# Linear attention with a routed expert layer: pairs of chunks, values held twice, and the next head's projection in alternating steps

## The chip, the cores and the metric

The kernel runs on one core of one Trainium2 chip. The metric is the device time of one execution in microseconds (us); the time before is the median of three runs. In the profile PE is the matmul engine (TensorE), PEld its weight loads, DVE VectorE, ACT ScalarE, POOL GpSimd, and SP (SyncE) a queue that issues most of the DMAs.

## The reference

One transformer layer on 2048 tokens of 512 numbers, in float32: a linear attention with 16 query heads in groups of four that share a key and a value head, and then a mixture of 32 experts, to which each token is sent by its eight best router choices.

```python
x = layernorm(x0)
q = rope(x @ Wq.T)            # 16 heads of 128
k = rope(x @ Wk.T)            # 4 heads of 128, each shared by 4 query heads
v = x @ Wv.T
qf, kf = elu(q) + 1, elu(k) + 1
for s in range(2048):         # a running state for each head
    state += kf[s][:, None] * v[s][None, :]
    z     += kf[s]
    out[s] = (qf[s] @ state) / (qf[s] @ z + 1e-6)
x1 = x0 + out @ Wo.T
# experts: softmax of the router's 64 logits, top 8 with a bias; of these, numbers below 32
# are experts with at most 256 tokens each (silu(gate) * up, then down), the others add
# their weight to a factor on the sum
return x1 + moe(layernorm(x1))
```

## The kernel before, in words

The first part, attention, takes about 885 of the 1235 us; the second, the experts, is not touched by the change.

The 2048 tokens are cut into four blocks `sb` of 512, each block into four chunks `c` of 128, each chunk into two halves of T = 64. The heads are worked off in four groups `g`; "head" below means such a group, one key head with its R = 4 query heads.

For each block the rows are normalised and transposed to `xT` (`norm_block`, transposes `pxt` at L262), and at g = 0 the values are projected for all four chunks (`values`, `pv` at L271, copied to `va` on ACT).

`project(sb, g, xT)` makes one head's inputs. The key projection is four matmuls into `pk` (L305), and `rope_feature` (L282 to L288) applies the rotation and elu + 1: five steps on DVE, an exponential on ACT (L287), one more step on DVE. `zT` is the running sum of the keys by a scan on DVE (L309). The four query projections `pq` (L317) follow, each with a `rope_feature`. Keys and queries share the two PSUM banks of `p_pj`. Then the denominators: DVE multiplies queries by `zT` (`qz`, L325), PE sums these into `pd` (L328), DVE adds 1e-6 and takes the reciprocal (`rd`, L331 and L332). They are needed along all partitions, so `rd` is stored to DRAM (`recip`, L333) and loaded back in four pieces, one per chunk, repeated for each partition (`rds`, L337). Both DMAs are issued by SP. `rds` has three buffers.

`attend(sb, g, c, ...)` works one chunk of one head:

- `by_token` has turned the keys to tokens by rows (transposes `pk` at L294, copied to `kk`).
- Scores `psc` of the two halves (L355) and new state terms `pst` (L361). The second state contains the first half's term, so the first matmul contracts over 64 rows and the second over 128. Both lie in one bank `psk`.
- DVE adds the old state (L366) and masks the scores to `at` (L370).
- For each half `po` is first the state times the queries (L376) and then the values times `at` (L379).
- DVE multiplies `po` by `rds` into `oT` (L381).

`output` multiplies the four `oT` of a chunk by `wo` (16 matmuls, `px`, L391) and adds the residual; `route` computes the router's logits, the top eight, and the ranks of the tokens in their experts by a matmul `pp` (L446 and L447), and `list_further` writes the token lists by indirect DMAs on POOL (L166).

The order of issue is written out in the loop at the end. At head g the whole projection of head g + 1 is issued first, then the four chunks of head g. At g = 3 the "next head" is head 0 of the next block, and the outputs and routes of earlier chunks stand between the chunks. [...] A scheduler may move instructions of independent parts against each other on an engine before they are fixed, so that parts of a chunk's work and of the projection stand among each other on PE and DVE.

Of the kernel before, what the change touches and what calls it, by code (L numbers as in the profile page):

```python
# [9 lines left out]
F32 = mybir.dt.float32  # L10
# [3 lines left out]
ALU = mybir.AluOpType  # L14
# [4 lines left out]
P = 128  # L19
# [3 lines left out]
G = 4  # L23
R = H // G
T = 64
# [27 lines left out]
def linattn_moe(  # L53
# [122 lines left out]
    with ExitStack() as ph:  # L176
        wts = ph.enter_context(tc.tile_pool(name="wts", bufs=1))
        blk = ph.enter_context(tc.tile_pool(name="blk", bufs=2))
# [3 lines left out]
        rdp = ph.enter_context(tc.tile_pool(name="rdp", bufs=NC - 1))  # L182
        rowp = ph.enter_context(tc.tile_pool(name="rowp", bufs=NC))
        vap = ph.enter_context(tc.tile_pool(name="vap", bufs=NC))
# [6 lines left out]
        p_sc = ph.enter_context(tc.tile_pool(name="p_sc", bufs=2, space=PSUM))  # L191
# [73 lines left out]

        def values(sb, c, xT):

            pv = p_pj.tile([P, G, HD], F32, tag="pj", name=f"pv_{sb}_{c}")
            pvf = pv.rearrange("p g d -> p (g d)")
            for k in range(KD):  # L270
                nc.tensor.matmul(pvf, lhsT=xT[:, k, ts(c, P)], rhs=wv[:, k, :],  # L271
                                 start=(k == 0), stop=(k == KD - 1))
            va = vap.tile([P, G, HD], F32, tag="va", name=f"va_{sb}_{c}")
            nc.scalar.copy(va, pv)
            return va
# [23 lines left out]
        def project(sb, g, xT):  # L299


            kT = qkp.tile([P, SB], F32, tag="kT", name=f"kT_{sb}_{g}")
            pk = p_pj.tile([P, SB], F32, tag="pj", name=f"pk_{sb}_{g}")
            for k in range(KD):
                nc.tensor.matmul(pk, lhsT=wk[:, k, ts(g, HD)], rhs=xT[:, k, :],  # L305
                                 start=(k == 0), stop=(k == KD - 1))
            rope_feature(kT, pk, sb, f"k{sb}_{g}")
            zT = zp.tile([P, SB], F32, tag="zT", name=f"zT_{sb}_{g}")
            nc.vector.tensor_tensor_scan(zT, ones[:, 0:1].to_broadcast([P, SB]), kT,  # L309
                                         zend[:, g : g + 1] if sb else 0.0, ALU.mult, ALU.add)  # L310
            if sb < NSB - 1:
                nc.scalar.copy(zend[:, g : g + 1], zT[:, SB - 1 :])
            qT = qkp.tile([P, R, SB], F32, tag="qT", name=f"qT_{sb}_{g}")
            for r in range(R):
                pq = p_pj.tile([P, SB], F32, tag="pj", name=f"pq_{sb}_{g}_{r}")
                for k in range(KD):
                    nc.tensor.matmul(pq, lhsT=wq[g][:, k, ts(r, HD)], rhs=xT[:, k, :],  # L317
                                     start=(k == 0), stop=(k == KD - 1))
                rope_feature(qT[:, r, :], pq, sb, f"q{sb}_{g}_{r}")

            pd = p_ms.tile([P, P], F32, tag="ms", name=f"pd_{sb}_{g}")
            for c in range(NC):
                cc = ts(c, P)
                qz = tmp.tile([P, R, P], F32, tag="qz", name=f"qz_{sb}_{g}_{c}")
                nc.vector.tensor_tensor(qz, qT[:, :, cc], zT[:, cc].unsqueeze(1).to_broadcast([P, R, P]),  # L325
                                        ALU.mult)
                for r in range(R):
                    nc.tensor.matmul(pd[ts(r, SL)], lhsT=pick[:, c, :], rhs=qz[:, r, :],  # L328
                                     start=(c == 0), stop=(c == NC - 1))
            rd = sml.tile([P, P], F32, tag="rd", name=f"rd_{sb}_{g}", bufs=1)  # L330
            nc.vector.tensor_scalar(rd, pd, 1e-6, None, ALU.add)  # L331
            nc.vector.reciprocal(rd, rd)  # L332
            nc.sync.dma_start(out=recip[sb][g].rearrange("r m t -> (r m) t"), in_=rd)  # L333
            rds = []
            for c in range(NC):
                t = rdp.tile([P, R, P], F32, tag="rds", name=f"rds_{sb}_{g}_{c}")
                nc.sync.dma_start(out=t, in_=recip[sb][g][:, c, :].unsqueeze(0).to_broadcast([P, R, P]))  # L337
                rds.append(t)
            return kT, qT, rds
# [3 lines left out]
        def attend(sb, g, c, proj, kk, va, oT):  # L343


            kT, qT, rds = proj
            n = f"{sb}_{g}_{c}"
            halves = range(P // T)
            half = [slice(c * P + a * T, c * P + (a + 1) * T) for a in halves]
            old = state[g]  # L350
            psk = p_sc.tile([P, R * T + 2 * HD], F32, tag="sc", name=f"psk_{n}")
            psc = psk[:, : R * T].rearrange("p (r t) -> p r t", r=R)
            pst = psk[:, R * T :].rearrange("p (a d) -> p a d", a=2)
            for a in halves:
                nc.tensor.matmul(psc[ts(a, T)], lhsT=kT[:, half[a]], rhs=qT[:, :, half[a]],  # L355
                                 start=True, stop=True)

            n_new = 2 if sb < NSB - 1 or c < NC - 1 else 1
            for a in range(n_new):
                to = slice(0, (a + 1) * T)  # L360
                nc.tensor.matmul(pst[:, a], lhsT=kk[to, c], rhs=va[to, g, :], start=True, stop=True)  # L361
            new = stp.tile([P, 2, HD], F32, tag=f"st{g}", name=f"state_{n}")
            if old is None:
                nc.vector.tensor_copy(new, pst)
            else:
                nc.vector.tensor_tensor(new[:, :n_new], pst[:, :n_new],  # L366
                                        old[:, 1:].to_broadcast([P, n_new, HD]), ALU.add)
            state[g] = new
            at = tmp.tile([P, R, T], F32, tag="at", name=f"at_{n}")
            nc.vector.tensor_tensor(at, psc, causal.unsqueeze(1).to_broadcast([P, R, T]), ALU.mult)  # L370
            pos = []
            for a in halves:
                po = p_o.tile([P, R, T], F32, tag=f"o{a}", name=f"po_{n}_{a}")
                before_half = (old[:, 1] if old is not None else None, new[:, 0])[a]
                if before_half is not None:
                    nc.tensor.matmul(po, lhsT=before_half, rhs=qT[:, :, half[a]], start=True, stop=False)  # L376
                pos.append((po, before_half is None))
            for a, (po, first) in enumerate(pos):
                nc.tensor.matmul(po, lhsT=va[ts(a, T), g, :], rhs=at[ts(a, T)], start=first, stop=True)  # L379
            for a, (po, first) in enumerate(pos):  # L380
                nc.vector.tensor_tensor(oT[:, :, half[a]], po, rds[c][:, :, ts(a, T)], ALU.mult)  # L381
# [22 lines left out]
        def route(ch, xw):  # L404
# [19 lines left out]
            sb_ = sml.tile([P, EZ], F32, tag="sbias", name=f"sbias_{ch}")  # L424
# [3 lines left out]
            rest = sml.tile([P, EZ], F32, tag="rest", name=f"rest_{ch}")  # L428
# [22 lines left out]
            if ch >= LISTED:  # L451

                free = sml.tile([P, E], F32, tag="hi", name=f"free_{ch}")
# [15 lines left out]
            hi = sml.tile([P, E], F32, tag="hi", name=f"hi_{ch}")  # L469
            nc.vector.tensor_scalar(hi, pos, float(C2), float(P * NCOL - 1), ALU.is_ge, ALU.mult)  # L470
            mi = sml.tile([P, E], F32, tag="mi", name=f"mi_{ch}")
            nc.vector.scalar_tensor_tensor(mi, pos, float(SL), off_2, ALU.is_ge, ALU.mult)
            ad = sml.tile([P, E], F32, tag="ad", name=f"ad_{ch}")
# [3 lines left out]
            ok = sml.tile([P, E], F32, tag="ok", name=f"ok_{ch}")  # L477
# [20 lines left out]
        projs = {(0, 0): project(0, 0, xTs[0])}  # L498
        oTs = {}
        waiting = []  # L500
        for sb in range(NSB):
# [3 lines left out]
            for g in range(G):  # L505
                if g == 0:
                    vas = [values(sb, c, xTs[sb]) for c in range(NC)]
                if g + 1 < G:
                    projs[sb, g + 1] = project(sb, g + 1, xTs[sb])
                elif not last:  # L510
                    xTs[sb + 1] = norm_block(sb + 1)
                    projs[sb + 1, 0] = project(sb + 1, 0, xTs[sb + 1])
                if last and g == G - 1:
                    for i in range(2):
                        load_pair(i)
                oT = otp.tile([P, R, SB], F32, tag="oT", name=f"oT_{sb}_{g}")
                oTs[sb, g] = oT
                kk = by_token(sb, g, projs[sb, g][0])
                for c in range(NC):
                    attend(sb, g, c, projs[sb, g], kk, vas[c], oT)  # L520
                    if g == G - 1:
                        if c != 1 and waiting:
                            route_and_list(*waiting.pop(0))
                        if c >= 1:
                            waiting.append((sb * NC + c - 1,
                                            output(sb, c - 1, [oTs[sb, i] for i in range(G)])))
# [23 lines left out]
        big = sml.tile([P, 2, 2, E // 2], F32, tag="big", name="big")  # L550
# [299 lines left out]
```

## Time and profile before

| | us |
|---|---|
| median of 3 runs | 1238.45 |
| lowest and highest of them | 1237.87 and 1241.02 |
| the profiled execution: its own time | 1237.05 |
| the profiled execution: span from first to last instruction | 1235.3 |
| PE busy in that span | 1050.5 |
| DVE busy | 637.9 |
| POOL busy | 219.7 |
| ACT busy | 130.2 |

The profile comes from one execution. Its page cuts the span into 40 slices of about 31 us and gives for each the busy share of every engine and the clock that was granted to TensorE. Windows give the same for any stretch; the timeline lists instructions with start and length, like ones put together with a count; the waits are listed by engine and line with what each wait ended on. L12 is line 12 of the kernel; the kernel after the change has other line numbers.

### The profile page before, as it was taken

What the parts mean: (1) busy time and instruction counts of PE and PEld (TensorE: products, weight loads), DVE (VectorE), ACT (ScalarE), POOL (GpSimd) and SP (SyncE); (2) the same over time, 40 slices, a digit from 0 to 9 for tenths busy, and PEclk for the clock granted to TensorE, in tenths of its full rate; (3) what the DMA queues carried; (4) which work ended last, traced back from release to release, by engine and by line L of the source; (5) the groups of instructions that cost most, each with busy time, mean ns of one, the idle gap of its engine ahead of it and who ended that gap; (6) DMA issues with size and microseconds to landing.
All of it is one profiled execution on the core that took longest, in us unless ns stands there. A gap on an engine that the chain in (4) does not pass through costs nothing. (4 is left out here: it accounts for less than half of the span.)

```text
span 1235.3 us, 13580 instructions
## 1 busy us (share of the span) xinstructions
PE 1050.5 (85%) x4410; PEld 530.9 (43%) x4410; DVE 637.9 (52%) x1553; ACT 130.2 (11%) x256; POOL 219.7 (18%) x254
## 2 busy tenths in 40 slices
PE   5999999999999899999999999999737765672772
PEld 2444444444444444444444444444312554441440
DVE  4888874358888435888843388834322111110110
ACT  1111110011121001112100111100011100110000
POOL 4000001430000343000034200023353121211211
PEclk9999999999999999999999999999967877786887
DMA  9411212100121210012321112340572484967224
GB/s 346 151 16 33 69 49 55 52 26 13 34 77 40 60 52 27 13 35 58 75 61 52 61 45 67 102 59 27 167 254 74 109 273 149 319 187 235 45 39 156
DMA packets 90840, 116.26 MB, mean 94 GB/s; under 512 B 12493, under 2 KB 47309, under 8 KB 90672
## 3 DMA queue, kind: packets, MB, share of 16 engines
q1 hardware_dynamic: 74640, 93.53, 25.5%
q0 software_dynamic: 10336, 12.51, 5.2%
q10 hardware_dynamic: 5760, 8.92, 2.0%
q8 instruction: 55, 0.90, 0.3%
q14 instruction: 49, 0.40, 0.1%
HBM read 101.35 MB, written 20.96 MB: 99 GB/s over the span
## 5 line engine op out<-in xcount | busy, mean ns | idle before, releaser
L317 PE MATMUL pq<-xT,wq 128*128 128x512 f32 x512 | 230.3, 599 | 10.1 <-DVE rb_q L284 10.1
L391 PE MATMUL px<-wo,oT 128*128 128x512 f32 x512 | 232.4, 599 | 0.0
L166 POOL DMA_INDIRECT slots<-tok,ai x120 | 117.6, 980 | 501.5 <-DVE ai L485 468.9
L317 PEld LDWEIGHTS pq<-xT,wq 128*128 128x128 f32 x512 | 94.4, 190 | 138.5 <-issue 107.3
L391 PEld LDWEIGHTS px<-wo,oT 128*128 128x128 f32 x512 | 93.9, 191 | 98.1 <-issue 97.6
L728 PE MATMUL pu<-xeT,gu 128*128 128x224 f32 (+1 forms) x352 | 69.4, 367 | 11.0 <-DVE xeT L656 9.7
L376 PE MATMUL po<-qT,state 128*128 128x256 f32 x248 | 76.8, 402 | 2.2 <-DVE oT L381 1.9
L728 PEld LDWEIGHTS pu<-xeT,gu 128*128 128x128 f32 x352 | 65.4, 230 | 15.4 <-issue 13.1
L393 DVE TENSOR_TENSOR x<-px,x 128x512 f32<-128x512 f32 x16 | 11.1, 692 | 113.6 <-PE px L391 98.8
L381 DVE TENSOR_TENSOR oT<-po,rds 128x256 f32<-128x256 f32 x128 | 50.1, 414 | 33.7 <-PE po L379 18.8
L305 PE MATMUL pk<-xT,wk 128*128 128x512 f32 x128 | 63.5, 627 | 0.7 <-ACT xT L263 0.7
L242 POOL TENSOR_TENSOR lnr<-lnv,mhalf 128x1 f32<-128x1 f32 (+1 forms) x20 | 13.3, 664 | 255.0 <-DVE lnv L240 228.8
L271 PE MATMUL pv<-wv,xT 128*128 128x512 f32 x128 | 57.7, 598 | 0.0
L361 PE MATMUL psk<-va,kk 64*128 64x128 f32 (+1 forms) x248 | 56.7, 323 | 0.0
L287 ACT ACTIVATE rb_q<-rb_q 128x512 f32<-128x512 f32 x64 | 40.3, 630 | 155.4 <-DVE rb_q L286 155.1
L376 PEld LDWEIGHTS po<-qT,state 128*128 128x128 f32 x248 | 41.2, 189 | 35.6 <-issue 21.7
L379 PE MATMUL po<-at,va 64*128 64x256 f32 x256 | 54.6, 428 | 0.0
L355 PE MATMUL psk<-qT,kT 128*64 128x256 f32 x256 | 50.5, 404 | 0.0
L361 PEld LDWEIGHTS psk<-va,kk 64*128 64x128 f32 (+1 forms) x248 | 36.8, 186 | 31.6 <-issue 23.8
L643 POOL DMA_INDIRECT acc<-y,idx x17 | 25.9, 1524 | 130.0 <-ACTq L778 40.0
L672 PE MATMUL pu_b<-gu,xeT_b 128*32 128x256 f32 x512 | 40.2, 424 | 10.0 <-issue 9.5
L325 DVE TENSOR_TENSOR qz<-qT,zT 128x512 f32<-128x512 f32 x64 | 42.4, 687 | 11.1 <-PE pd L328 10.6
(180 smaller groups left out, 1135.1 us busy)
## 6 DMA issues: line engine op xcount, KB each, us to landing
gu<-in_wgu_dram SPq DMA_DIRECT2D x32, 1024.0 KB
rds<-recip SPq DMA_DIRECT2D x64, 256.0 KB
dn<-in_wdn_dram SPq DMA_DIRECT2D x32, 512.0 KB
rows<-xw ACTq DMA_DIRECT2D x16, 272.0 KB
xn<-in_x_dram SPq DMA_DIRECT2D x16, 256.0 KB
wq<-in_wqT_dram SPq DMA_DIRECT2D x4, 1024.0 KB
wo<-in_woT_dram SPq DMA_DIRECT2D x4, 1024.0 KB
x<-in_x_dram SPq DMA_DIRECT2D x16, 256.0 KB
```

Of the source, the lines that this page charges most:

```text
L166: nc.gpsimd.indirect_dma_start(out=slots[k][:, :], out_offset=bass.IndirectOffsetOnAxis(ap=ai[:, k : k + 1], axis=0), in_=tok[:, ch : ch + 1],
L271: nc.tensor.matmul(pvf, lhsT=xT[:, k, ts(c, P)], rhs=wv[:, k, :], start=(k == 0), stop=(k == KD - 1))
L305: nc.tensor.matmul(pk, lhsT=wk[:, k, ts(g, HD)], rhs=xT[:, k, :], start=(k == 0), stop=(k == KD - 1))
L317: nc.tensor.matmul(pq, lhsT=wq[g][:, k, ts(r, HD)], rhs=xT[:, k, :], start=(k == 0), stop=(k == KD - 1))
L325: nc.vector.tensor_tensor(qz, qT[:, :, cc], zT[:, cc].unsqueeze(1).to_broadcast([P, R, P]), ALU.mult)
L355: nc.tensor.matmul(psc[ts(a, T)], lhsT=kT[:, half[a]], rhs=qT[:, :, half[a]], start=True, stop=True)
L361: nc.tensor.matmul(pst[:, a], lhsT=kk[to, c], rhs=va[to, g, :], start=True, stop=True)
L376: nc.tensor.matmul(po, lhsT=before_half, rhs=qT[:, :, half[a]], start=True, stop=False)
L379: nc.tensor.matmul(po, lhsT=va[ts(a, T), g, :], rhs=at[ts(a, T)], start=first, stop=True)
L381: nc.vector.tensor_tensor(oT[:, :, half[a]], po, rds[c][:, :, ts(a, T)], ALU.mult)
L391: nc.tensor.matmul(px, lhsT=oTs[h // R][:, h % R, ts(c, P)], rhs=wo[h // R][:, h % R, :], start=(h == 0), stop=(h == H - 1))
L728: nc.tensor.matmul(pu[:, a, :m], lhsT=weights[e][0][:, k, a, c, :], rhs=xeT[:, k, :m], start=(k == 0), stop=(k == KD - 1))
```

## The change

- *Pairs of chunks.* `attend` becomes `attending`, a generator that works two chunks together in two steps. The first step issues the four score matmuls of both chunks into one bank, the two state matmuls into another, the two additions of the state and the two masks. The second step issues the four matmuls of state times queries, the four of values times `at`, and the four multiplications by `rds`. `po` now holds both chunks.
- *Values held twice.* `vas` holds for each chunk and head two copies of the values side by side, of which the first has zeros in rows 64 to 127. One matmul of 128 x 256 then gives both states of a chunk. The zeros are written once, the copies by two ACT instructions per chunk.
- *Alternating steps.* `project` becomes `projecting`, a generator of six steps: key, four queries, denominators. The loop issues a step of the present head's pairs, then one or more of the next head's projection, and so on. The outputs and routes at g = 3 stand between these steps too.
- *Buffers.* cos and sin one instead of two; `rds` two instead of three; values one for each chunk, twice as large; scores one bank instead of two, and a new bank for the states; several small tiles of `route` one instead of two.

In the changed kernel the lines are: key transposes L299, key projection L310, scan L314, query projection L323, `qz` L332, `pd` L335, `rd` L338 and L339, store L340, load L344, scores L363, states L368, state addition L374 and L376, mask L382, `po` L390 and L395, `oT` L399, `px` L411, `pp` L466 and L467.

```diff
-        blk = ph.enter_context(tc.tile_pool(name="blk", bufs=2))
+        blk = ph.enter_context(tc.tile_pool(name="blk", bufs=1))
-        rdp = ph.enter_context(tc.tile_pool(name="rdp", bufs=NC - 1))
+        rdp = ph.enter_context(tc.tile_pool(name="rdp", bufs=2))
-        vap = ph.enter_context(tc.tile_pool(name="vap", bufs=NC))
+        vap = ph.enter_context(tc.tile_pool(name="vap", bufs=1))
-        p_sc = ph.enter_context(tc.tile_pool(name="p_sc", bufs=2, space=PSUM))
+        p_sc = ph.enter_context(tc.tile_pool(name="p_sc", bufs=1, space=PSUM))
+        p_st = ph.enter_context(tc.tile_pool(name="p_st", bufs=1, space=PSUM))
...
+        vas = [vap.tile([P, G, 2, HD], F32, name=f"va_{c}") for c in range(NC)]
+        for va in vas:
+            nc.gpsimd.memset(va[T:, :, 0, :], 0.0)
...
-            nc.scalar.copy(va, pv)
-            return va
+            nc.scalar.copy(vas[c][:, :, 1, :], pv)
+            nc.scalar.copy(vas[c][:T, :, 0, :], pv[:T])
...
-        def project(sb, g, xT):
+        def projecting(sb, g, xT):
...
+            yield
             qT = qkp.tile([P, R, SB], F32, tag="qT", name=f"qT_{sb}_{g}")
             for r in range(R):
...
                 rope_feature(qT[:, r, :], pq, sb, f"q{sb}_{g}_{r}")
+                yield
...
-            return kT, qT, rds
+            projs[sb, g] = kT, qT, rds
+            yield
...
-        def attend(sb, g, c, proj, kk, va, oT):
+        def attending(sb, g, c0, proj, kk, oT):
...
+            psc = p_sc.tile([P, 2, R, T], F32, tag="sc", name=f"psc_{n}")
+            for i in chunks:
+                for a in halves:
+                    nc.tensor.matmul(psc[ts(a, T), i], lhsT=kT[:, half[i][a]], rhs=qT[:, :, half[i][a]],
+                                     start=True, stop=True)
+
+            pst = p_st.tile([P, 2, 2, HD], F32, tag="st", name=f"pst_{n}")
+            for i in chunks:
+                nc.tensor.matmul(pst[:, i], lhsT=kk[:, c0 + i], rhs=vas[c0 + i][:, g], start=True, stop=True)
...
+                    nc.vector.tensor_tensor(new, pst[:, i], old[:, 1:].to_broadcast([P, 2, HD]), ALU.add)
...
+                nc.vector.tensor_tensor(at, psc[:, i], causal.unsqueeze(1).to_broadcast([P, R, T]), ALU.mult)
+                ats.append(at)
+            yield
+            po = [p_o.tile([P, 2, R, T], F32, tag=f"o{a}", name=f"po_{n}_{a}") for a in halves]
+            fresh = [True, True]
+            for i in chunks:
+                for a in halves:
+                    if seen[i][a] is not None:
+                        nc.tensor.matmul(po[a][:, i], lhsT=seen[i][a], rhs=qT[:, :, half[i][a]],
+                                         start=fresh[a], stop=False)
+                        fresh[a] = False
+            for i in chunks:
+                for a in halves:
+                    nc.tensor.matmul(po[a][:, i], lhsT=vas[c0 + i][ts(a, T), g, 1, :], rhs=ats[i][ts(a, T)],
+                                     start=False, stop=(i == 1))
+            for i in chunks:
+                for a in halves:
+                    nc.vector.tensor_tensor(oT[:, :, half[i][a]], po[a][:, i], rds[c0 + i][:, :, ts(a, T)],
+                                            ALU.mult)
+            yield
...
-        projs = {(0, 0): project(0, 0, xTs[0])}
+        projs = {}
+        for _ in projecting(0, 0, xTs[0]):
+            pass
...
-                if g + 1 < G:
-                    projs[sb, g + 1] = project(sb, g + 1, xTs[sb])
-                elif not last:
-                    xTs[sb + 1] = norm_block(sb + 1)
-                    projs[sb + 1, 0] = project(sb + 1, 0, xTs[sb + 1])
...
+                if g + 1 < G:
+                    ahead = projecting(sb, g + 1, xTs[sb])
+                elif not last:
+                    xTs[sb + 1] = norm_block(sb + 1)
+                    ahead = projecting(sb + 1, 0, xTs[sb + 1])
+                else:
+                    ahead = iter(())
...
-                for c in range(NC):
-                    attend(sb, g, c, projs[sb, g], kk, vas[c], oT)
-                    if g == G - 1:
-                        if c != 1 and waiting:
-                            route_and_list(*waiting.pop(0))
-                        if c >= 1:
-                            waiting.append((sb * NC + c - 1,
-                                            output(sb, c - 1, [oTs[sb, i] for i in range(G)])))
+                pairs = [attending(sb, g, c, projs[sb, g], kk, oT) for c in (0, 2)]
...
+                next(pairs[0])
+                next(ahead, None)
+                next(pairs[0])
+                if g == G - 1:
+                    routed()
+                next(ahead, None)
+                if g == G - 1:
+                    put(0)
+                next(ahead, None)
+                next(pairs[1])
+                if g == G - 1:
+                    routed()
+                    put(1)
+                next(ahead, None)
+                if g < G - 1:
+                    next(ahead, None)
+                next(pairs[1])
+                if g == G - 1:
+                    next(ahead, None)
+                next(ahead, None)
+                if g == G - 1:
+                    routed()
+                    put(2)
```

`routed` takes the oldest waiting chunk through `route` and `list_further`, if there is one; `put` issues a chunk's `output` and puts the chunk on the waiting list. The last chunk of a block is output after the loop over the heads, as before.

## The prediction

> **What bounds the kernel now.** I read the page's slices first: TensorE (PE) at 9 tenths and full clock to slice 28, the attention part (0 to about 885 us); behind it the expert part, which the diff leaves alone. Then windows cut from one group of key transposes (L294) to the next give one head each; columns are length, busy time of PE, PEld, DVE, ACT, POOL, clock, DMA share, GB/s.
> ```profile
> 319.40:352.70 33.30, 32.80 (x141) 15.37 (x140) 29.07 (x54) 3.92 (x7) 0.00 (x0) 1.00 0.14 34
> 352.70:388.50 35.80, 34.26 (x157) 16.95 (x156) 28.69 (x54) 6.27 (x11) 0.00 (x0) 1.00 0.29 76
> 388.50:502.60 114.10, 109.64 (x366) 52.21 (x365) 59.33 (x199) 9.86 (x19) 34.61 (x37) 1.00 0.14 39
> ```
> A head of 33.3 us has PE busy for 32.8, but VectorE (DVE) for 29.1: PE leads by under 4 us. The long window is head 3 with its outputs. So a PE saving in heads 0 to 2 is worth little before DVE takes over. The timeline of PE in the first window:
> ```profile
> 321.11 0.90 PE L361 MATMUL psk<-va,kk 64*128 64x128 f32 x4
> 326.72 0.70 PE L376 MATMUL po<-qT,state 128*128 128x256 f32 x2
> 333.69 1.03 PE L376 MATMUL po<-qT,state 128*128 128x256 f32 x4
> 334.65 0.70 PE L379 MATMUL po<-at,va 64*128 64x256 f32 x4
> ```
> Last, the denominators: DVE makes rd, SyncE (SP) stores it (L333) and loads it back in four pieces (L337), by which DVE multiplies the outputs (L381).
> ```profile
> 49.96 0.33 SPq L333 DMA_DIRECT2D recip<-rd  x1
> 51.72 1.47 SPq L337 DMA_DIRECT2D rds<-recip  x3
> 363.59 0.38 SPq L337 DMA_DIRECT2D rds<-recip  x1
> 371.50 0.76 DVE L381 TENSOR_TENSOR oT<-po,rds 128x256 f32<-128x256 f32 x2 [2.66 <-DMA rds<-recip]
> DVE oT L381 <- DMA rds<-recip: 14.7, 7, 5.1
> ```
> (The last: us in total, times, longest.) Store to first load 1.76 us (3.0 at 155, 3.8 at 193 us); a load issued at 363.59 is used at 371.50, 7.9 later (8.0 at 117.7, 7.9 at 330.7). Before, this seldom hurts: a head's projection stands a whole head ahead of its attention, and only the fourth piece, for want of a buffer, is loaded late.
>
> **What the Trainium skill says.** (1) "Perfetto Trace Analysis", section "DMA Instruction — HWDGE (DVE, Sync)": a DMA's profiled time is its issue, the movement lies outside it. The trace agrees: 0.38 us shown, 7.9 to use. (2) "TensorE: Matmul & The Clock Gate", table at its head: VectorE's queue is strict FIFO. Agrees: at 371.50 DVE sat 2.66 us, and the rope behind came after. So a wait for a denominator holds all later ropes. (3) Same page, "Part 1: The HAM clock gate": after an idle window of about 3.4 us the clock halves. Partly: a gap of 2.89 us ending at 637 was followed by clocks 0.63 and 0.50 for some 3 us, one of 3.27 us at 420 was not. (4) "TensorEngine Tiling (Array Packing)", "Key Properties": changing the tiling mode drains TensorE. Agrees in direction: two L376 alone take 0.53 to 0.63 us start to start, four in a run 0.96 to 1.07.
>
> **The change, part by part.**
> *State matmuls.* 248 of N=128 (four take 0.83 us here, 49.9 us in all) become 128 of N=256. No row shows this full-height form for the product; L376 (128x256) is nearest, 0.48 each in a run of two to four: 31 us, a saving of 19. Bounds 10 to 25.
> *Scores, and outputs in runs of four.* Scores 45.2 to about 35; state part of the outputs 68.2 to 56; L379 58.2 to 35 (four in 0.63 against a lone pair in 0.62). Saving 10, 12, 23. With the states: 64 us of PE, 4 per head; bounds 40 to 75. In heads 0 to 2 PE then needs 33 - 4 = 29 us.
> *DVE.* Same work: five ropes at 3.7 to 3.9 (18.8), scan 1.28, four qz at 0.69 (2.7), rd 1.2, four states 1.7, four at 1.65, eight oT 3.3, hence 30.6, and 0.76 behind an exponential: about 31.2. DVE becomes the bound, and head 0 falls from 33.5 to 31.2.
> *Values twice.* 16 more copies on ACT, 4 memsets on POOL. ACT is busy 3.9 of 33 us; nothing while that idle time stands, else 16 x 0.6 = 10 us at most.
> *Projection in alternating steps.* This takes away the head of slack. In the compiled order, head g+1's rd is DVE's work directly ahead of g+1's own first pair, and that pair's oT stand ahead of the four q ropes of head g+2. Count from the last rope of g+1 (t=0). oT of the earlier pair 1.5, qz 2.7, rd 1.2: rd done at 5.4. Store to load 1.8 to 3.0: load issued at 7.2 to 8.4. Landing +7.9: 15 to 16.3. The second piece is issued 0.5 later and shares the rate; three together (339 us on) took some 12, so I put it 9 to 10 after the first issue: 16.5 to 18.4, taken 17.5. DVE meanwhile does two states and two at (1.6), the k rope with its exponential (4.5) and scan (1.3), and stands at its oT at 12.8. It idles to 17.5, 4.7 us in two steps (bounds 2.5 and 7). Behind it: last two oT 0.8, four ropes 14.8, pair 1's states and at 1.7, exponentials about 2: 36.8 (35.5 to 38.5) against 33.3. PE has po, two q projections and the next pair in hand, then fills both banks of p_pj and waits; its saved 4 us become idle time.
> So in each block: head 0 (denominators stored early, during the outputs) -2.3; head 1 +3.5; head 2 36.8 to 37.8 against 35.8, +1.5. Sum +2.7.
> *Head 3* holds 16-matmul outputs of 13.7 us each and is PE's: -4. Its first outputs need little of head 3's own oT. But a waiting chunk's route now stands between: pp (L466) stands in PE's order ahead of later px matmuls and needs sel from DVE, which is held by the denominators (4.7) and then does its chain of small steps: 5 to 7 us of PE waiting, and about 2 if the clock halves. Block 0 has no waiting chunk at first: -2.2. Blocks 1 and 2: -4 + 6 + 2 = +4. Block 3: +4, and on SP a 1 MB expert load, which waits for a weight's buffer, now stands ahead of head 2's store: about 4 or 5 more, +9 (0 to +14).
> *Single cos/sin.* The next block's loads wait for the last rope of the block and are needed some 8 us later, at its first k rope after normalisation and transposes (window 352.7). They land, I estimate from the 7.9 above, just in time; otherwise 0 to 4 us, three times. *One p_sc bank* waits for at, already done; nothing, up to 0.5 per pair if DVE is late. *One buffer for rank tiles*: same engine, in order; nothing.
> Sum: block 0 +0.5, blocks 1 and 2 +6.7 each, block 3 +11.7: +25.6. The expert part starts later and is unchanged. Profiled execution: 1237.05 + 25 = 1262; it lies 1.4 below the median of the runs, 1238.45, which I leave in the range.
>
> **The rivals.**
> A, above: the denominators' trip decides, 1245 to 1282. For it: 7.9 us is measured on loads that were alone. Against it: the trip may be shorter on an idle queue.
> B, worse: PE's new gaps reach the length that halved the clock at 637. Two or three gaps a block at half clock for 4 us each add 2 us each, 20 us in all: 1282 to 1300. Against it: one gap of 3.27 us did no harm.
> C, **faster**: the pieces are there when DVE comes. It decides if the second lands by 12.8 after the last rope, so if rd to landing is under 7.4 us instead of 12. Then heads 0 to 2 are DVE's at about 31.2 (-2.3, -2.1, -2 or more) and head 3 PE's (-4): about 10 a block, 1237 - 40 = 1197; with half the stall, 1215 to 1230. For it: 64 us of PE work really go. Against it: wherever the use shows the landing, it came 7.8 to 8.8 after the issue.
> D, they cancel: stalls of about 2 us a head, 1235 to 1242.
> That the change doesn't do what it says: the four-matmul runs might be split again by the order and PE save under 30 us. With DVE as the bound that alone moves heads by little.
>
> **How the numbers follow.** A 0.60, B 0.08, C 0.25, D 0.07. A measurement of this kernel can tell 0.3%, 3.7 us. Faster 0.25, same 0.07, slower 0.68. The likeliest, A, gives 1262, with 1245 to 1282 for itself. The range leaves out the better half of C and most of B: 1212 to 1285.
>
> **What would show it.** Right: in the waits, DVE at the oT multiply (L399) for rds, some 12 stretches of 3 to 6 us, 50 us or more in all; windows of heads 1 and 2 at 36 to 38 us with PE busy 29 and DVE 30 to 31; of head 0 at about 31; PE waiting at the q projection (L323) for DVE's rope; groups L368 at 31 us, L395 at 35. Wrong: rds waits under 2 us each (then C), PE still 98% busy in heads 1 and 2 (then the saving was mis-sized), PEclk below 0.9 inside the heads (B), head 3 shorter than 110 us in blocks 1 and 2 (then the route coupling is not there).

## The result and the profile after

The changed kernel takes 1271.72 us (median of 4 runs, 1268.36 to 1274.13) against 1238.62 for the kernel before (4 runs, the three of above and one more): a ratio of 1.0262, 95% interval 1.0230 to 1.0294. It is slower, by 33 us; the forecast was 1262. The profiled execution took 1268.36 us, 31.3 above that of before.

All of this arises in the attention part. In PE's timeline the last px group ends at 887.3 us before and at 918.2 after, 30.9 later; from there to the end of the span it is 348.0 us before and 348.1 after. Below, "end of attention" is this point.

The waits of the changed kernel (engine, line, what ended the wait: us in total, times, longest):

```profile
DVE oT L399 <- DMA rds<-recip: 61.6, 21, 5.3
...
PE pq L323 <- DVE rb_q L289: 39.8, 9, 6.5
DVE xw L421 <- POOL lnr L243: 38.8, 12, 8.4
...
DVE oT L399 <- PE pq L323: 13.1, 3, 4.4
```

In the kernel before, the first line was 14.7 us. The last one belongs to it, which makes 75 us: that instruction needs `po` and `rds`, and its `po` was done at 307.43, long before. The listed L323 is only the last thing that PE did before the wait ended; with ones in place of `rds` (first experiment) the same instruction starts 6 us before that group of query projections ends. The timelines of SP, DVE and PE at head 1 of block 1 show it (start, length, engine, instruction, idle time before it):

```profile
303.98 0.95 DVE L339 RECIPROCAL rd<-rd 128x128 f32<-128x128 f32 x1
...
304.96 0.33 SPq L340 DMA_DIRECT2D recip<-rd  x1
306.51 12.06 SPq L344 DMA_DIRECT2D rds<-recip  x4
...
314.56 0.42 DVE L399 TENSOR_TENSOR oT<-po,rds 128x256 f32<-128x256 f32 x1 [4.38 <-PE pq L323]
...
317.43 0.76 DVE L399 TENSOR_TENSOR oT<-po,rds 128x256 f32<-128x256 f32 x2 [0.94 <-DMA rds<-recip]
318.10 0.68 DVE L287 TENSOR_TENSOR qT<-pq,cs 128x512 f32<-128x512 f32 x1
...
320.24 10.10 PE L323 MATMUL pq<-xT,wq 128*128 128x512 f32 x16 [3.67 <-DVE rb_q L289]
```

`xN` counts like instructions that follow each other. The four loads of L344 are such a group: its 12.06 us run from the first issue to the last, and the third and fourth wait for a buffer to come free. The denominators are ready at 304.93, the first load is issued at 306.51 and used at 314.56, 8.05 us later; both buffers were free, so no buffer holds this load. The first rope of the queries, at 318.10, stands behind both waits. PE has filled its two banks and idles 3.67 us for that rope, and its next 16 records (eight matmuls; one in f32 shows as two records here) take 10.1 us in place of 7.1. The windows between key transposes, columns as before (heads 1, 2 and 3 of block 1, then head 2 of block 3):

```profile
295.90:333.90 38.00, 34.15 (x135) 16.41 (x133) 29.76 (x55) 3.93 (x7) 0.00 (x0) 0.91 0.15 30
333.90:379.40 45.50, 38.74 (x191) 19.22 (x190) 35.16 (x66) 6.79 (x12) 0.00 (x0) 0.92 0.29 57
379.40:492.30 112.90, 106.61 (x351) 51.70 (x347) 59.80 (x198) 10.52 (x21) 30.75 (x33) 0.98 0.16 45
...
784.30:823.40 39.10, 32.61 (x133) 15.95 (x132) 28.38 (x53) 3.74 (x6) 0.00 (x0) 0.91 0.29 85
```

Head 1 grows from 33.3 to 38.0 us with 29.8 us of DVE work in it, and the mean clock of heads 1 and 2 falls to 0.91 and 0.92. Head 2 seems to lose more than it did: 66 DVE instructions lie in its window, 54 before, since the key transposes of head 3 now stand behind that head's first steps. Part of the work has moved across the mark, so only whole blocks compare. From last rope to last rope, heads 1 and 2 take 37.7 and 38.1 us.

### The profile page after: what moved, and what is told of

Read it like the earlier page. It is cut to its first block, busy times and chain, and to the rows that moved or that the text cites. A ratio compares the mean times of both kernels' runs of the same rounds, so it can differ in the third digit from the quotient of the medians.

```text
span 1266.3 us, 13329 instructions
## 1 busy us (share of the span) xinstructions
PE 1031.1 (81%) x4290; PEld 533.6 (42%) x4290; DVE 639.1 (50%) x1553; ACT 136.8 (11%) x272; POOL 221.9 (18%) x258
## 5 line engine op out<-in xcount | busy, mean ns | idle before, releaser
L323 PE MATMUL pq<-xT,wq 128*128 128x512 f32 x512 | 248.0, 638 | 39.8 <-DVE rb_q L289 39.8
L411 PE MATMUL px<-wo,oT 128*128 128x512 f32 x512 | 235.1, 609 | 0.2 <-DVE oT L399 0.2
L323 PEld LDWEIGHTS pq<-xT,wq 128*128 128x128 f32 x512 | 102.2, 205 | 167.8 <-issue 118.2
L411 PEld LDWEIGHTS px<-wo,oT 128*128 128x128 f32 x512 | 95.9, 194 | 106.5 <-issue 105.2
L399 DVE TENSOR_TENSOR oT<-po,rds 128x256 f32<-128x256 f32 x128 | 50.4, 418 | 75.4 <-DMA rds<-recip 61.6
L310 PE MATMUL pk<-xT,wk 128*128 128x512 f32 x128 | 67.4, 632 | 0.7 <-ACT xT L264 0.7
L390 PE MATMUL po<-qT,state 128*128 128x256 f32 x248 | 64.7, 390 | 1.5 <-DVE state L376 1.3
L390 PEld LDWEIGHTS po<-qT,state 128*128 128x128 f32 x248 | 44.8, 189 | 26.8 <-issue 16.8
L293 DVE SCALAR_TENSOR_TENSOR qT<-qT,rb_q 128x512 f32<-128x512 f32 x64 | 44.2, 690 | 9.4 <-ACT rb_q L292 6.9
L287 DVE TENSOR_TENSOR qT<-pq,cs 128x512 f32<-128x512 f32 x64 | 43.7, 683 | 4.2 <-PE pq L323 3.9
L288 DVE TENSOR_TENSOR rb_q<-pq,sn 64x512 f32<-64x512 f32 x64 | 44.4, 693 | 1.2
L332 DVE TENSOR_TENSOR qz<-qT,zT 128x512 f32<-128x512 f32 x64 | 41.9, 687 | 5.5 <-PE pd L335 5.1
L290 DVE TENSOR_TENSOR qT<-qT,rb_q 128x512 f32<-128x512 f32 x64 | 44.0, 688 | 1.2
```

What stands on the lines that cost most here:

```text
L287: nc.vector.tensor_tensor(dst, ps, cs, ALU.mult)
L288: nc.vector.tensor_tensor(b[:hh], ps[hh:], sn[hh:], ALU.mult)
L290: nc.vector.tensor_tensor(dst, dst, b, ALU.add)
L293: nc.vector.scalar_tensor_tensor(dst, dst, 0.0, b, ALU.max, ALU.add)
L390: nc.tensor.matmul(po[a][:, i], lhsT=seen[i][a], rhs=qT[:, :, half[i][a]], start=fresh[a], stop=False)
L399: nc.vector.tensor_tensor(oT[:, :, half[i][a]], po[a][:, i], rds[c0 + i][:, :, ts(a, T)], ALU.mult)
```

## The experiments

Ratios are to the kernel before, in runs on the same chip; times differ by about 1% from chip to chip. Windows, waits and ends of attention are those of one profiled execution of each kernel.

**The denominators taken away.**

```diff
-                    nc.vector.tensor_tensor(oT[:, :, half[i][a]], po[a][:, i], rds[c0 + i][:, :, ts(a, T)],
-                                            ALU.mult)
+                    nc.vector.tensor_tensor(oT[:, :, half[i][a]], po[a][:, i],
+                                            ones[:, :T].unsqueeze(1).to_broadcast([P, R, T]), ALU.mult)
```

> The outputs are multiplied by ones in place of the denominators, which are still made, stored and loaded but read by nobody (so the division is left out, and the router sees other rows; the expert part is not comparable, read the time at the end of the last px, 918 us in the changed kernel). Theory, the denominators' trip holds VectorE: the waits for rds (61.6 us listed, and 13.1 put down to pq) are gone, heads 1 and 2 fall from 38 to 31 to 33 us, the attention part ends at 865 to 880. Rival, the alternating steps themselves make PE and VectorE wait for each other: PE still waits 30 us or more at the q projections for the rope, and the end stays above 905.

The kernel leaves the division out. Attention ends at 833.2 us, 85 before the changed kernel and 54 before the old one; head 1 takes 31.1 us; no wait for rds is listed, and PE's wait at the query projection is 0.6 us in all, from 39.8. That is more than expected, and 10 us more than the 75 us of listed waits. PE's gaps and its lower clock went with them; which part of the 10 us is theirs isn't priced. DVE in block 1, at the place of the wait above (the pq group on PE ends at 299.97 here):

```profile
293.66 0.42 DVE L399 TENSOR_TENSOR oT<-po,ones 128x256 f32<-128x256 f32 x1
```

**Pairs in the old order.** The loop runs all of `ahead` first, then both pairs; everything else is as in the changed kernel, save that at head 3 two routes now stand behind the second pair, with only an output between them.

```diff
-                next(pairs[0])
-                next(ahead, None)
-                next(pairs[0])
...
+                for _ in ahead:
+                    pass
+                for c in range(2):
+                    for _ in pairs[c]:
+                        pass
+                    if g == G - 1:
+                        routed()
+                        put(0 if c == 0 else 1)
+                        if c == 1:
+                            routed()
+                            put(2)
```

> Pairs, values held twice and all the new buffer sizes stay; only the order of issue goes back to a whole projection ahead of the present head's chunks. Theory: the denominators again have a head of slack, waits for rds under 20 us in all; VectorE bounds heads 0 to 2 at 31 to 32 us and PE head 3, total 1198 to 1215. Rival, the smaller buffers (two rds, one bank of scores, one cos and sin) cost the time: total 1238 or more, with waits at those tiles.

1279.70 us, 1.0317 (1.0271 to 1.0362): a miss. The order was thought to restore the slack, but the waits for rds are 78.2 us. SP and DVE show why:

```profile
301.91 1.89 SPq L344 DMA_DIRECT2D rds<-recip  x2
...
309.93 0.42 DVE L399 TENSOR_TENSOR oT<-po,rds 128x256 f32<-128x256 f32 x1 [1.70 <-DMA rds<-recip]
...
314.21 1.09 DVE L399 TENSOR_TENSOR oT<-po,rds 128x256 f32<-128x256 f32 x3 [3.86 <-DMA rds<-recip]
```

With two buffers the second pair's pieces are loaded when the first pair's are used (301.91), and in this order the second pair follows at once: its first piece is used 8.0 us after the issue, its second later still. The head of slack serves only the first pair's pieces, and those are there in time.

**The old kernel with two buffers** (`rdp` bufs from 3 to 2, nothing else).

> The kernel before with one edit: two buffers for rds in place of three. Theory, from the run of pairs in the old order: with two buffers the third piece too is loaded only when the first is used, some 8 us before its own turn; waits for rds grow from 14.7 to 50 us or more and the time to 1250 to 1280. Rival, the third buffer is idle slack: time within 5 us of 1238.

1279.36 us, 1.0402 (1.0343 to 1.0460), waits for rds 60.1 us. So the old order needs its third buffer. In the changed kernel the second pair of heads 1 to 3 of block 1 waits for no piece with two buffers: half a projection lies between its pairs. Pairs in the old order with three buffers, and the changed kernel with three, were not run.

**Alternating steps alone.** The old kernel with single chunks and all its buffers, its projection cut into the same steps: chunk, k, chunk, q, q, chunk, q, q, chunk, denominators.

> The kernel before (single chunks, all its buffer sizes) with the projection's steps between its chunks in the same places: chunk 0, k, chunk 1, q, q, chunk 2, q, q, chunk 3, denominators. Theory: the waits for rds come back without any pair, 75 us or more in all, since a head's denominators are again made just ahead of their use; with no PE saving in head 3 the total is 1275 to 1310. Rival, it takes the pairs (two chunks' outputs waiting at once) to make the loss: total within 10 us of 1238.

1269.52 us, 1.0226 (1.0182 to 1.0271), end of attention 917.4. Waits for rds 54.2 us, fewer than expected, and a few us faster than the range; but the loss is there without a pair or a doubled value, and pairs on top change the end little (918.2). The order makes the loss.

**Outputs later.**

```diff
                 next(pairs[0])
                 next(ahead, None)
-                next(pairs[0])
                 if g == G - 1:
                     routed()
                 next(ahead, None)
+                if g < G - 1:
+                    next(ahead, None)
+                next(pairs[0])
                 if g == G - 1:
                     put(0)
-                next(ahead, None)
+                    next(ahead, None)
                 next(pairs[1])
```

> As the changed kernel, with one move: the output step of the first pair stands behind the first two q projections (at head 3 behind the first) in place of behind the k projection. Theory: VectorE comes to oT some 7 us later, about 19 us after the last rope, when both pieces have landed (15.5 and 18.4); waits for rds fall from 75 to under 20 us, heads 1 and 2 to 32 or 33, total 1205 to 1225. Rival, alternating steps as such cost: total stays above 1255.

1220.03 us, 0.9814 (0.9771 to 0.9858): one step moved turns the loss into a gain. 39.9 us of waits for rds are left, more than expected, in block 1 all of them at the second pair, whose pieces are loaded at the first pair's later use. The longest there, 3.93 us at 355.99, came 13.8 us after the piece's issue, and the next block's cosine, sine and first rows were issued on the same queue in between (348.03 to 350.78).

**Single chunks without denominators**, to price the pairs: the edit of the first experiment in the kernel of single chunks and alternating steps.

> The kernel with single chunks in alternating steps, with ones in place of the denominators as before (the division is left out; read the end of the last px, not the total). It prices the pairs once no wait for denominators is left: the same with pairs ended at 833 us. Theory, the pairs and doubled values save PE some 64 us, but VectorE takes over in heads 0 to 2: the end lies at 850 to 875, heads 1 and 2 at 33 to 34 us against 31.0, head 3 four or more us longer. Rival, the pairs save PE nothing where it matters: the end within 8 us of 833.

Attention ends at 852.9 us, against 833.2 with pairs: the pairs are worth 19.7 us once no output waits for a piece. Head 1 takes 32.0, less than expected, and 31.1 with pairs; the head is PE's in this kernel, busy for all of its 32.0 us.

**Denominators spread by PE.** No store and no load; a column of the identity as weights copies a row of rd to all partitions.

```diff
...
+            for r in range(R):
+                row = r * SL + c
+                nc.tensor.matmul(pb[:, r, :], lhsT=ident[:, row : row + 1].to_broadcast([P, P]), rhs=rd,
+                                 start=True, stop=True)
+            t = rdp.tile([P, R, P], F32, tag="rds", name=f"rds_{sb}_{g}_{c}")
+            nc.scalar.copy(t, pb)
...
```

> The changed kernel and its order, but the denominators are not stored and loaded: PE spreads a row of rd over all partitions by a matmul with a column of the identity (16 of 128x128 per head, about 2 us of PE), ACT copies it to rds just ahead of its use. Theory, the trip is what costs: no waits for rds, heads 1 and 2 at 31 to 33 us, attention ends at 835 to 860, total 1188 to 1213, faster than the kernel before by 2 to 4%. Rival, the alternating order costs by itself (PE waits for ropes and ropes for PE): total above 1235.

1230.58 us, 1.0015 (1.0003 to 1.0028; the kernel before took 1228.85 on this chip). Faster than the changed kernel, as expected, but no faster than before: a miss. The waits are gone (3.9 us are left, for ACT). What was wrong is the price: a window of head 1 and the spread in PE's timeline,

```profile
299.40:333.60 34.20, 33.41 (x167) 18.70 (x165) 29.18 (x53) 6.16 (x11) 0.00 (x0) 1.00 0.00 0
```
```profile
308.99 1.05 PE L348 MATMUL pb<-rd,ident 128*128 128x128 f32 x8
309.88 1.03 PE L396 MATMUL po<-qT,state 128*128 128x256 f32 x4
```

One such matmul in f32 is two records here (256 of them are 512 records), eight records take 0.89 us start to start, and a head needs 32: 3.6 us of PE, 57 us in 16 heads, where 2 a head were assumed. Attention ends 58.6 us after that of the kernel with ones. PE, with 33.4 busy of 34.2, is the bound.

**The same in the old order.**

> As e7_spread_by_pe, with a whole projection ahead of the present head's pairs (the order of the kernel before). Theory: with the trip gone the order matters little, total within 15 us of e7_spread_by_pe. Rival, the alternating steps were worth something by themselves: e7 is faster by 20 us or more; or they were harmful, then this one is faster by as much.

1264.31 us, 1.0295 (1.0266 to 1.0323): 34 us slower than in alternating steps, so the first rival holds: the steps, with the place of the routes that comes with them, are worth something. One part can be named. At head 3 of block 1 POOL issues two token lists, 16 indirect DMAs 1.28 us apart, and only then comes the power that the next normalisation waits for:

```profile
457.91 0.97 POOL L166 DMA_INDIRECT slots<-tok,ai  x1 [0.30 <-issue]
...
458.89 0.58 POOL L243 TENSOR_TENSOR lnr<-lnv,mhalf 128x1 f32<-128x1 f32 x1
...
459.51 0.55 DVE L427 TENSOR_SCALAR xw<-x,mv,lnr 128x512 f32<-128x512 f32 x1 [8.56 <-POOL lnr L243]
...
460.20 1.09 PE L434 MATMUL prt<-ident,xw 128*128 128x128 f32 x4 [8.54 <-DVE xw L427]
```

PE stood 8.54 us here in block 1 and 8.53 in block 2. The rest of the 34 isn't assigned.

**Pieces in whole rows.** The layout of `recip` in DRAM becomes chunk, head, token, so that a partition reads 2048 bytes in one stretch, not four of 512. Rows r * 32 + c of rd go there in four small stores.

```diff
-    recip = [[dram.tile([R, SL, P], F32, name=f"recip_{sb}_{g}") for g in range(G)] for sb in range(NSB)]
+    recip = [[dram.tile([NC, R, P], F32, name=f"recip_{sb}_{g}") for g in range(G)] for sb in range(NSB)]
...
-            nc.sync.dma_start(out=recip[sb][g].rearrange("r m t -> (r m) t"), in_=rd)
+            for r in range(R):
+                nc.sync.dma_start(out=recip[sb][g][:, r, :], in_=rd[r * SL : r * SL + NC, :])
...
-                nc.sync.dma_start(out=t, in_=recip[sb][g][:, c, :].unsqueeze(0).to_broadcast([P, R, P]))
+                nc.sync.dma_start(out=t, in_=recip[sb][g][c].unsqueeze(0).to_broadcast([P, R, P]))
```

> The changed kernel and its order; only the layout of recip in DRAM differs: chunk, head, token in place of head, chunk, token, so that a piece is 2048 bytes in a row for each partition (128 packets of 2 KB) in place of four stretches of 512 bytes (512 packets). The store becomes four small ones, one per head. Theory, the trip is long because packets of a load start at only some 84 per us while the engines are idle: 128 packets take 1.5 us in place of 6, a piece lands 3.5 to 5 us after its issue, later by about 1 us for the four stores; waits for rds fall from 75 to under 25 us, heads 1 and 2 to 31 to 34 us, total 1190 to 1220. Rival, the trip is a fixed delay of DRAM and semaphores, or bound by bytes: landing stays at 7 to 8 us and the total within 8 us of 1272.

1187.01 us, 0.9567 (0.9537 to 0.9597). No wait for rds is listed at all; attention ends at 834.3, within 1.1 us of the kernel that doesn't use them. SP, DVE and the window of head 1 in block 1:

```profile
289.87 1.27 SPq L341 DMA_DIRECT2D recip<-rd  x4
292.14 6.51 SPq L345 DMA_DIRECT2D rds<-recip  x4
...
296.31 0.73 DVE L400 TENSOR_TENSOR oT<-po,rds 128x256 f32<-128x256 f32 x2
...
297.56 0.75 DVE L400 TENSOR_TENSOR oT<-po,rds 128x256 f32<-128x256 f32 x2
```
```profile
280.80:311.90 31.10, 30.91 (x135) 15.41 (x133) 28.68 (x54) 3.94 (x7) 0.00 (x0) 1.00 0.10 35
```

DVE uses the first piece 4.2 us and the second 5.4 us after the first issue without idling. The stores are smaller too (16 rows for 128), but the times compared here run from the first load's issue, after the stores. The DMA view of the changed kernel from 306 to 318 us (slices of 0.3 us: busy tenths of the engines, GB/s) and of this one from 292 to 298 (slices of 0.15):

```profile
DMA  1000011111211111979223459652100111111001
GB/s 50 0 0 0 0 41 44 44 38 46 44 46 38 44 44 43 39 32 48 20 46 41 73 149 196 97 120 63 46 29 26 44 43 46 39 43 34 0 26 43
DMA packets 1137, 0.56 MB, mean 47 GB/s; under 512 B 44, under 2 KB 1137, under 8 KB 1137
```
```profile
DMA  0000000246464789998643200000000000000000
GB/s 0 0 0 0 0 0 0 96 150 218 164 177 123 205 287 341 341 369 328 246 191 150 96 14 0 0 0 0 0 0 0 0 0 0 0 0 0 0 0 0
DMA packets 288, 0.52 MB, mean 87 GB/s; under 512 B 32, under 2 KB 32, under 8 KB 288
```

About the same bytes move. In packets of 512 bytes they flow at some 44 GB/s for about 5 us, in the first 3 of them with the engines at one tenth busy, and after that faster; in packets of 2 KB at 96 to 369 GB/s, and all is moved in 2.5 us. 44 GB/s are 86 packets of 512 bytes per us. The packets of 2 KB start at a mean of 162 GB/s in their first seven slices, which is 79 packets per us: at first both start at about the same number per us, whatever they hold. It is no fixed ceiling, for from 312.6 to 314.4 us packets of 512 bytes flow at 63 to 196 GB/s. What sets the rate no run shows; that longer stretches shorten the trip is shown.

**Whole rows and later outputs.**

> e4_outputs_later (first pair's outputs behind two q projections) with the same layout of recip. Theory: its remaining waits, 39.9 us, mostly for the second pair's pieces, go too; total 1185 to 1205, at most 10 us better than e11_whole_rows, since both then have next to no wait for rds. Rival (landing unchanged): total stays at 1220.

1185.89 us, 0.9550 (0.9519 to 0.9581): the same as without the later step. With nothing to wait for, this shift of the outputs is worth nothing.

**Whole rows in the old kernel, and in pairs in the old order.**

> The kernel before with the same layout of recip. Theory: it waits for rds only 14.7 us, and PE bounds it, so it gains at most that: 1224 to 1238. Rival, the layout helps every kernel alike, by 40 us or more, and says nothing on the change.

> e2_pairs_old_order (pairs, doubled values, two rds buffers, a whole projection ahead) with the layout of recip by chunk. It prices the alternating steps once the trip is short, against e11_whole_rows (0.957 of the kernel before). Theory: with a short trip the order is worth little in heads 0 to 2, waits for rds under 15 us in all, and head 3 pays for two token lists that stand one behind the other on POOL (8.5 us a block in the run of the spread): total 1195 to 1225. Rival: two buffers in this order still hold VectorE, total above 1240.

1233.31 us, 0.9929 (0.9904 to 0.9954), and 1209.26, 0.9749 (0.9711 to 0.9787), both totals as expected, and neither lists a wait for rds. The reason given for the second isn't seen: no wait of PE at the router's transposes (`prt`) is longer than 3.4 us in it, where 8.5 us a block were expected. The ends of attention side by side, with 512-byte stretches and with the trip short (* with ones):

| | old order, 512 B | alternating, 512 B | old order, short | alternating, short |
|---|---|---|---|---|
| single chunks | 887.3 | 917.4 | 882.2 | 852.9* |
| pairs, values twice | 926.7 | 918.2 | 863.4 | 834.3 |

With the trip short both parts of the change are gains and add up: pairs 19, alternating steps 29 us. The 29 us price the order together with the place of the routes, which changes with it; for pairs some 25 of them lie in blocks 0 to 2 (5, 9 and 11 us), and what makes them isn't assigned. With the long trip the alternating steps are a loss alone, and pairs on top are no better. The 926.7 is not the loss of the pairs: they stand with two rds buffers, single chunks with three, and single chunks with two end at 937.8 (1.0402). The runs come from several chips, but the difference between chips seems to lie behind attention: from the end of attention to the end of the span it is 337.0 to 338.5 us in the three runs with denominators on the chip of 1228.85, and 344.4 to 351.2 in all other runs with denominators.

## Why the prediction was right, point by point

The case was A: DVE held by denominators that are on their way. Taking them away, delaying their use, replacing the trip and shortening it each removed the loss; alternating steps alone brought it. The rivals that need no trip (steps that make PE and DVE wait for each other, pairs that bring the loss) are excluded by the same runs.

- **The trip.** Forecast from the last rope: rd at 5.4 us, store to load 1.8 to 3.0, landing 7.9, second piece at 17.5. In the head shown above (last rope ends at 299.03): 5.9, 1.55, 8.05, 18.4. DVE stood at the outputs at 11.2, not 12.8, since the first of them comes ahead of the scan. It waited 5.3 us (6.0 in head 2); forecast 4.7. The waits came in head 3 of each block too, 75 us in 12 heads, where 50 or more were given as the sign. From rope to rope 37.7 and 38.1; forecast 36.8, and 36.8 to 37.8.
- **Blocks.** Between the first key transposes of each block: 0.0, +7.8, +7.1, and +16.0 for the last (200.5 against 166.5, less the 18.1 by which the first mark of all lies earlier, one projection less being done by then). Forecast +0.5, +6.7, +6.7, +11.7. Of the 5 us that the sum is too small, 4 lie in the last block.
- **The forecast of the bound was wrong, its size small.** DVE was to take over in heads 0 to 2, at 31.2 us, with PE at 29. With the trip short a head takes 31.1 us, but PE is busy for 30.9 of it and DVE for 28.7. Two terms failed. DVE's durations were added, but neighbours overlap: two oT of 0.42 take 0.76. And PE's saving was put at 64 us, where the four groups went from 238.6 to 184.1 busy, 54.5; it stays inside the bounds. The four sums that it starts from (49.9, 45.2, 68.2 and 58.2) stand in no view; the view by lines has 56.7, 50.5, 76.8 and 54.6 busy. States, scores and the state part of the outputs saved 21, 7 and 12 (forecast 19, 10 and 12); L379 saved 14 where 23 was forecast, and holds most of the difference.
- **Head 3.** The forecast of 5 to 7 us was for the wait at a route's ranks (`pp`). That was 2.14 us in block 1; another 3.30, which the forecast doesn't name, were waited for its logits (`pl`). The sum fits, in part by luck. The clock there stayed at 0.98, so the 2 us for it were not due.
- **Block 3.** The cause that was forecast was wrong, and that its sum came near is luck. The expert load did not delay head 2's store, which went out 0.03 us after rd (794.58, 794.61); its first load came 3.4 us later, where 1.55 is usual, for a reason that stays open. The larger part lies in the tail, which has no next projection. DVE's wait held the end of a route, so POOL got its list late, and the power behind it. PE stood 8.87 us, where the kernel with whole rows has at most 2.3 us at this line in its tail:

```profile
847.03 0.76 DVE L399 TENSOR_TENSOR oT<-po,rds 128x256 f32<-128x256 f32 x2 [2.83 <-DMA rds<-recip]
...
849.47 0.97 POOL L166 DMA_INDIRECT slots<-tok,ai  x1 [129.21 <-DVE ai L505]
...
859.38 0.60 POOL L243 TENSOR_TENSOR lnr<-lnv,mhalf 128x1 f32<-128x1 f32 x1
...
860.61 1.11 PE L428 MATMUL prt<-ident,xw 128*128 128x128 f32 x4 [8.87 <-issue]
```

- **Rival B** came true in part: in heads 1 and 2 PE had gaps of 3.7 to 6.5 us, and the 16 records of query projections behind each took 8.65 to 10.20 us in place of 7.1; the sign given, a clock below 0.9 inside the heads, was just missed (0.91). In the stretch looked at this cost little, since DVE was the one behind: from 320 to 327 us, at a clock of 0.55, it was busy for 6.44 of 7.0 us.
- **Rival C**, at 1197, is the kernel with whole rows, at 1187. Its condition, rd to the second piece in under 7.4 us, was missed by the change (12.5: 304.93 to 317.43) and met there: rd is done at 289.84, the DMA view has all of both pieces moved by 295.6, and the outputs wait for neither.
- **Edits costed at nothing** (single cos and sin, copies on ACT, single rank tiles) show no wait of a reader on PE or DVE; weight loads waited 1.7 us in all behind the copies.

## What to carry to other kernels

An order that saves work on the bounding engine can use up the slack that hid a trip through DRAM; count the time from the last producer to the first consumer in the new order, and what stands behind the consumer on its engine. Before such an order is given up, look at the trip: here the length of a contiguous stretch turned 1.026 into 0.957. And a buffer count is right only for one order and one length of the trip: with the long trip single chunks in the old order waited 60.1 us with two buffers and 14.7 with three; with the short one pairs in that order list no wait with two.

## What the runs showed of the hardware

A DMA of 256 KB in stretches of 512 bytes was used 8.05 us after its issue by an engine that stood waiting for it; for about 5 us it flowed at some 44 GB/s, for 3 of them with the DMA engines at a tenth busy. In stretches of 2048 bytes two such loads were used 4.2 and 5.4 us after the first issue, without a wait. A column of the identity, repeated with a stride of zero, serves as weights that spread a row over all partitions, at 0.22 us for 128 x 128 in f32 (0.89 us for four).
